# A selective scan's outputs written back into the gathered rows' tiles, and the last token rows through three tiles

## The chip, the cores and the metric

The kernel runs on one core of a Trainium2 chip. The metric is the device time of one execution in microseconds (us). The engines are named as in the profile: PE (matrix multiply; PEld its weight loads), DVE, ACT, POOL, and SP, which here only issues DMAs.

## The reference, cut to what matters

Four residual layers act on one image x of 1024 channels and 64x64 pixels, in float32. Each layer adds f(groupnorm(x)) to x. Layer 0 is a layer norm with a decaying scan over the channels; layers 1 and 3 are 1x1 convolutions. Layer 2 is the one that matters here:

```
xz   = silu(in_proj_w @ x + b);  x_ssm, res, gate = split(xz, 3)
xf   = silu(depthwise_conv3(x_ssm))             # along the 4096 tokens
dbc  = dbc_w @ xf + dbc_b                       # per head: dt, B (8), C (8)
dt   = softplus(dbc[dt])
x_h, dt, B, C = each gathered by perm           # an order of tokens per head (argsort)
h_t  = exp(dt_t * A) * h_{t-1} + dt_t * B_t * x_t      # 2 heads, 8 states, 512 channels a head
y_t  = C_t . h_t + D * x_t
y    = y gathered by the inverse of perm
out  = silu(out_proj_w @ (y * silu(gate) + res) + b)
```

## The kernel before, in words

The 1x1 convolutions are products of 1024x1024 weights with 1024x4096 pixels. They are done by one or two steps of Strassen's scheme, which trades products for sums of weights (POOL) and of inputs (DVE, POOL).

**Up to 1124 us.** Layers 0 and 1 come first. From about 590 us PE does the x_ssm product (WX). Between its parts lie the convolution, the turning of tokens into rows and a sort of the tokens by their scan order. `turn` writes each token's 512 channels of a head into a table in device memory, `tok_d` (line 1098 and its neighbours). `finish(pair)` (line 1143) is called for each of four pairs of 8 blocks of 128 tokens. It makes dt by a softplus and multiplies B by it. Then it writes for four blocks at a time (TPB) the second part of each token's row into the tile `row`. There dt stands once, and B and C in split form: `hi` holds the upper 20 bits (line 1198), `lo` the rest (line 1200), each in two places, so that one product with both gives the full precision. The second places are copied by POOL (lines 1201 and 1202). SP then sends the rows to `tok_d` (lines 1204 to 1210). A token's row has 512 + NF2 = 656 floats. There is only one `row` tile, so the next four blocks can be written only when the transfer of the last has landed. `finish` is a generator: between its `yield`s the loop does a step of the product.

**1124 to 1142 us.** The last pair is finished without product steps between (`for _ in finish(NP - 1)`). It has a ninth, partial block for the very last token.

**1142 to 1657 us, the scan.** The 4096 tokens of a head are taken in 74 chunks of 56 (8 more rows carry the state). One chunk of both heads fills a tile g of 128 rows, from a pool with 6 buffers. `gather(k)` (line 1291, POOL) fetches the rows of chunk k from `tok_d` in scan order by an indirect DMA. For iteration k the engines get this order:

- PE: `turn_rows(k+1)` (lines 1305 and 1306) turns B and C and sums dt; then a unit of the `res` product (WR, line 839, eight matmuls); `apply(k-1)` (line 1344) multiplies the chunk's weights G with its rows; `cross(k)` (line 1327) multiplies B with C; maybe another unit.
- DVE: `weigh(k-1)` (lines 1335 to 1340) makes G; `spread_decay(k+1)` (lines 1312 to 1320); sums for the product (lines 797 and 1028).
- ACT: ds, the running sums' input for chunk k+2 (line 1299); copies of finished products (line 1024); in `apply`, the state rows into the next chunk's tile (line 1347) and y out of PSUM into a tile y (line 1349); `Exp` of the decay of chunk k+1 (line 1384); Silu of finished `res` parts (line 1034).
- POOL: `scatter(k-1)` (line 1353) sends y to `y_d` by an indirect DMA to the tokens' own places; `gather(k+5)`; sums of inputs (line 797) and of weights for the next stage (lines 468 to 488).

These orders are written out by hand, so an instruction that waits holds all behind it on its engine. A scatter waits for the copy of its y and for the scatter before to land, since both write `y_d`. There are two y tiles, so the copy of y(k) waits for scatter k-2 to land. PE's products of chunk k+1 wait for gather k+1 and for ds of it. The tile y of PSUM (py) is single, so `apply(k)` waits for the copy of y(k-1).

Of the `res` product 14 units come before the first chunk (`first`); the other 98 are spread evenly over the iterations. SP's loads and stores for the product, and for the sums of weights, stand in one queue.

**From 1657 us** PE does the remaining products: gate, out_proj and layer 3.

Of the kernel before, what the change touches and what calls it, by code (L numbers as in the profile page):

```python
# [9 lines left out]
F32 = mybir.dt.float32  # L10
# [9 lines left out]
P = 128  # L20
C = 1024
HW = 64
N = HW * HW
# [13 lines left out]
NK = -(-N // LT)  # L37
HS = HEADS * S
KW, MW = 4 * HS, 66
NF2 = 9 * HS  # L40
CF, BF, DT = 0, KW, 2 * KW
HI, LO = {CF: (0, 2), BF: (0, 1)}, {CF: (1, 3), BF: (2, 3)}
NSPEC = HEADS * S + 1

W1, WX, WR, WG, WO, W3 = range(6)
# [47 lines left out]
def tile_net(ctx: ExitStack, tc: tile.TileContext, x, par_d, cst_d, w_d, w2_d, dbcw_d, out):  # L93
# [137 lines left out]
    with tc.tile_pool(name="spec", bufs=1) as sp:  # L231
        rows = sp.tile([NSPEC, DH + NF2], F32, name="spec")
        nc.gpsimd.memset(rows, 0.0)
        for at in (BF, CF):
            for j in HI[at]:
                c = DH + at + j * HS
                nc.gpsimd.tensor_copy(rows[:HS, c : c + HS], ident[:HS, :HS])
        nc.sync.dma_start(tok_d[HEADS * N :, :], rows)
# [262 lines left out]


    mean0 = const.tile([P, CT], F32, name="mean0")
    sum0 = const.tile([P, CT, 2 * NPIECE], F32, name="sum0")
    sq0 = const.tile([P, CT, 2 * NPIECE], F32, name="sq0")
    with tc.issue_after(exp_ln.ins), tc.tile_pool(name="l0x", bufs=2) as lx, \
            tc.tile_pool(name="l0x2", bufs=1) as lx2, \
            tc.tile_pool(name="wsum0", bufs=1, side="right") as wsum0, \
# [30 lines left out]
        for t in range(T0):  # L539
            nc.gpsimd.tensor_scalar(dtm[:, t, :], cst[:, CST["row"]], pcol("dtw", t), None, ALU.mult)  # L540
        carry = l0.tile([P, 2, T0], F32, name="carry", bufs=1)
        nc.vector.memset(sum0, 0.0)
        nc.vector.memset(sq0, 0.0)
        nmean0 = l0.tile([P, CT], F32, name="nmean0", bufs=1)
# [494 lines left out]
    with tc.tile_pool(name="l2a", bufs=2) as pa, tc.tile_pool(name="l2a2", bufs=1) as pa2, \  # L1039
# [11 lines left out]
        def tok_rows(t0, q, n, c0, h):  # L1051
            return tok_d[h * N + t0 : h * N + t0 + q * P, c0 : c0 + n].rearrange("(q p) c -> p q c", p=P)
# [91 lines left out]
        def finish(pair):  # L1144
            n = 2 * TPB
            yield
            acc = accs[pair].rearrange("p b (h f) -> p b h f", h=HEADS)
            if pair == NP - 1:

                nc.vector.memset(acc[:, n], 0.0)  # L1150
                nc.scalar.activation(end, end, AF.Silu)
                pe = ps_tp("end_pt")
                nc.tensor.transpose(pe[:CT, :P], end, ident)
                et = pa.tile([CT, P], F32, name="end_t", bufs=1)
                nc.scalar.copy(et, pe[:CT, :P])
                for h in range(HEADS):
                    nc.sync.dma_start(tok_d[h * N + N - 1 : h * N + N, :DH].rearrange("a (b c) -> (a b) c", c=P),
                                      et[h * KH : (h + 1) * KH, :])
                pz = ps_tp("end_dbc")
                for o in range(CT):  # L1160
                    nc.tensor.matmul(pz[:1, : HEADS * NF], end[:, o : o + 1], both[:, o, P:], start=(o == 0), stop=(o == CT - 1))
                nc.vector.tensor_tensor(accs[pair][:1, n], pz[:1, : HEADS * NF], dbcb[:1], ALU.add)
                n += 1


            def t(name):
                w = pa.tile([P, 2 * TPB + 1, HEADS], F32, tag=f"sp_{name}", name=f"sp_{name}{pair}", bufs=1)
                return w[:, :n]

            f = acc[:, :n]  # L1170
            v, m, e, u, d = t("v"), t("m"), t("e"), t("u"), t("d")
            nc.vector.tensor_copy(v, f[:, :, :, 0])
            nc.vector.tensor_scalar(m, v, 0.0, None, ALU.max)
            nc.scalar.activation(e, v, AF.Abs)
            nc.scalar.activation(e, e, AF.Exp, scale=-1.0)

            nc.vector.tensor_scalar(u, e, 1.0, None, ALU.add)
            nc.vector.tensor_scalar(d, u, -1.0, None, ALU.add)
            nc.vector.tensor_tensor(d, e, d, ALU.subtract)
            nc.vector.reciprocal(v, u)  # L1180
            nc.vector.tensor_tensor(d, d, v, ALU.mult)
            nc.scalar.activation(u, u, AF.Ln)
            nc.vector.tensor_tensor(u, u, d, ALU.add)
            nc.vector.tensor_tensor(u, u, m, ALU.add)
            nc.vector.tensor_tensor(f[:, :, :, 1 : 1 + S], f[:, :, :, 1 : 1 + S],
                                    u.unsqueeze(3).to_broadcast([P, n, HEADS, S]), ALU.mult)
            for b0 in range(0, n, TPB):
                if b0:
                    yield
                q = min(TPB, n - b0)  # L1190
                nc.vector.tensor_copy(row[:, :q, :, DT], u[:, b0 : b0 + q])
                for h in range(HEADS):
                    for at, c in ((BF, 1), (CF, 1 + S)):
                        v = f[:, b0 : b0 + q, h, c : c + S]
                        parts = row[:, :q, h, at : at + KW].rearrange(
                            "p b (a c) -> p b a c", c=HS)[:, :, :, h * S : (h + 1) * S]
                        (hi, hi2), (lo, lo2) = ([parts[:, :, j] for j in which[at]] for which in (HI, LO))
                        nc.vector.tensor_scalar(hi.bitcast(I32), v.bitcast(I32), 12, 12, ALU.logical_shift_right,
                                                ALU.logical_shift_left)
                        nc.vector.tensor_tensor(lo, v, hi, ALU.subtract)  # L1200
                        nc.gpsimd.tensor_copy(hi2, hi)
                        nc.gpsimd.tensor_copy(lo2, lo)
                    t0 = pair * 2 * FB + b0 * P - 1
                    if t0 < 0:
                        nc.sync.dma_start(tok_d[h * N : h * N + P - 1, DH:], row[1:, 0, h, :])
                        nc.sync.dma_start(tok_rows(t0 + P, q - 1, NF2, DH, h), row[:, 1:q, h, :])
                    elif q < TPB:
                        nc.sync.dma_start(tok_d[h * N + N - 1 : h * N + N, DH:], row[:1, 0, h, :])
                    else:
                        nc.sync.dma_start(tok_rows(t0, q, NF2, DH, h), row[:, :q, h, :])  # L1210

        forget(LATE)
        with tc.manual_schedule(engines={E_.DVE, E_.PE, E_.Pool, E_.Activation}):
# [60 lines left out]

    with tc.tile_pool(name="l2r2", bufs=6) as prg, tc.tile_pool(name="l2g", bufs=6) as pgat, tc.tile_pool(name="l2b", bufs=2) as pb, tc.tile_pool(name="l2h", bufs=1) as ph, \
            tc.tile_pool(name="ps2b", bufs=1, space=PSUM) as psb:
        rg_pools[:] = [prg] * 6 + rg_pools * 4
        G2 = [ph.tile([P, P], F32, name=f"G{i}") for i in range(2)]  # L1280
# [60 lines left out]

        def apply(k):
            py = psb.tile([P, FB], F32, tag="y", name=f"py{k}")
            nc.tensor.matmul(py, G2[k % 2], rows.pop(k)[:, :DH], start=True, stop=True)  # L1344
            if k + 1 < NK:
                for h in range(HEADS):
                    nc.scalar.copy(rows[k + 1][h * LC : h * LC + S, :DH], py[h * LC : h * LC + S])  # L1347
            y = pb.tile([P, DH], F32, tag="y", name=f"y{k}")
            nc.scalar.copy(y, py)  # L1349
            return y  # L1350

        def scatter(k, y):
            nc.gpsimd.indirect_dma_start(  # L1353
                out=y_d[:, :], out_offset=bass.IndirectOffsetOnAxis(ap=dst_[:, k : k + 1], axis=0),
                in_=y[:, :], in_offset=None,
            )

        sums = (None for m in (WO, W3) for _ in sum_weights2(m, ph, nc.sync, 64, lag=(1, None)))
# [3 lines left out]

        pgs = {}
        with tc.manual_schedule(engines={E_.DVE, E_.PE, E_.Pool, E_.Activation}):
            while given < first:
                next_units(total)
            for k in range(5):
                gather(k)
            step_sums(0)
            for k in range(-1, NK + 1):  # L1370
                upto = first + (k + 2) * (total - first) // (NK + 2)
                turned = turn_rows(k + 1) if k + 1 < NK else None
                if k > 0:
                    weigh(k - 1, pgs.pop(k - 1))
                if turned is not None:
                    spread_decay(k + 1, *turned)
                if k + 2 < NK:
                    step_sums(k + 2)
                next_units(upto)
                y = apply(k - 1) if k > 0 else None  # L1380
                if 0 <= k < NK:
                    pgs[k] = cross(k)
                if k + 1 < NK:
                    nc.scalar.activation(decay_[k + 1], decay_[k + 1], AF.Exp)
                if y is not None:
                    scatter(k - 1, y)
                if 4 < k + 5 < NK:
                    gather(k + 5)
                next_units(upto)
                if given // 2 % 14 != 12:  # L1390
                    next(sums, None)
                if len(silus) > 3:
                    activate(4)
# [427 lines left out]
```

## Time and profile before

| | us |
|---|---|
| median of three runs | 2715.85 (2709.34 to 2719.6) |
| the profiled execution | 2721.77, span 2719.4 |
| PE busy in the span | 2577.5 |
| the stretch of the last pair of rows | 1124 to 1142 |
| the scan | 1142 to 1657 |

A line of waits gives an instruction, what released it, the total of its waits, how many there were and the longest. A timeline line gives the start, the duration, the engine, the line of the kernel, the operation with out<-in and, in brackets, how long the engine had stood idle before and what ended that. Where the named releaser had finished long before, another event of the same wait was the last one. A row of windows gives the busy time of each engine in a stretch, the clock that PE was granted (1.00 is full), and the share of time in which the DMA engines were busy.

### The profile page before, as it was taken

How to read it: one execution, taken by the hardware profiler on the slowest of the kernel's cores; microseconds unless marked ns; L12 is line 12 of the kernel's file. 1: busy time of each engine (PE TensorE's matmuls, PEld its weight loads, DVE VectorE, ACT ScalarE, POOL GpSimd, SP SyncE). 2: the span in 40 equal slices, each digit the busy share in tenths (PEclk: the TensorE clock that was granted, in tenths of full speed). 3: DMA queues.
4: the chain of work that ended last, by engine and by line, in shares of the span. 5: the costliest groups of instructions: out<-in, count | busy, mean ns of one | idle time of the engine just before them, and what ended most of it. 6: DMA issues, size and time to landing. Idle time of an engine off the chain costs nothing.

```text
span 2719.4 us, 30951 instructions
## 1 busy us (share of the span) xinstructions
PE 2577.5 (95%) x9520; PEld 1715.8 (63%) x9520; DVE 1824.2 (67%) x3870; ACT 1086.4 (40%) x1840; POOL 1223.9 (45%) x1166
## 2 busy tenths in 40 slices
PE   4788999999999999999999999999999999999999
PEld 3664444444555555444444447888888888788887
DVE  6996856655555644377777775577576686877777
ACT  3783110103646554375766554322233133321220
POOL 4154123232122220246585665566575565654544
PEclk9897999999999999999999999999999999999999
DMA  7245467546443363478888994879799898788896
GB/s 287 102 169 201 147 218 262 190 124 230 139 138 103 110 175 111 144 236 262 236 236 236 277 269 152 242 244 305 217 278 292 235 308 238 248 304 292 299 328 215
DMA packets 423577, 598.22 MB, mean 220 GB/s; under 512 B 141909, under 2 KB 211669, under 8 KB 420342
## 3 DMA queue, kind: packets, MB, share of 16 engines
q1 hardware_dynamic: 299062, 368.89, 42.3%
q10 hardware_dynamic: 91456, 136.33, 14.3%
q0 software_dynamic: 32896, 91.04, 12.9%
q8 instruction: 77, 1.26, 0.2%
q14 instruction: 86, 0.70, 0.1%
HBM read 435.63 MB, written 160.51 MB: 219 GB/s over the span
## 4 chain that ended last, share of the span: by engine, by line
PE 48%; DVE 3%; DMA 2%; issue 2%; ACT 2%; POOL 1%; SPq 0%; DVEq 0%; POOLq 0%; ACTq 0%
PE mm L839 8%; PE q_P2P L1695 5%; PE q_P6P L1695 5%; PE q_P5P L1695 5%; PE q_P3P L1695 5%; PE q_P7P L1695 5%; PE q_P1P L1695 5%; PE q_P4P L1695 5%; PE py L1344 2%; DMA y_d<-y,dst 1%; POOL s L468 1%; PE pr L1305 1%; DMA g<-tok_d,src 0%; DVE pg L1337 0%; DVE t L797 0%
## 5 line engine op out<-in xcount | busy, mean ns | idle before, releaser
L839 PE MATMUL mm<-t,w 128*128 128x512 f32 x1536 | 687.4, 598 | 9.3 <-ACT rg L1024 6.2
L839 PE MATMUL mm<-b,w 128*128 128x512 f32 x1152 | 518.7, 602 | 4.0 <-ACT b L943 2.9
L839 PEld LDWEIGHTS mm<-t,w 128*128 128x128 f32 x1536 | 287.4, 191 | 335.2 <-issue 315.6
L839 PEld LDWEIGHTS mm<-b,w 128*128 128x128 f32 x1152 | 218.0, 193 | 254.7 <-issue 243.7
L1664 ACT COPY qQ<-q_P5P 128x512 f32<-128x512 f32 x48 | 28.1, 585 | 294.9 <-PE q_P5P L1695 294.9
L1065 DVE SCALAR_TENSOR_TENSOR cvp<-xs,par,cvp 128x512 f32<-128x512 f32 x128 | 95.3, 754 | 71.7 <-ACT cvp L1062 69.4
L1353 POOL DMA_INDIRECT y_d<-y,dst x74 | 74.9, 1012 | 143.2 <-ACT y L1349 83.5
L468 POOL TENSOR_TENSOR s<-s 128x256 f32<-128x256 f32 (+3 forms) x120 | 130.0, 1090 | 7.9
L1092 POOL TENSOR_TENSOR acc<-l2xt,acc 128x136 f32<-128x136 f32 x56 | 27.2, 486 | 234.6 <-ACT l2xt L1086 233.6
L1116 DVE TENSOR_TENSOR xs<-mm,xs 128x512 f32<-128x512 f32 x64 | 41.9, 685 | 125.0 <-PE mm L839 125.0
L1347 ACT COPY g<-py 8x512 f32<-8x512 f32 x146 | 83.6, 573 | 77.4 <-PE py L1344 69.5
L958 DVE SCALAR_TENSOR_TENSOR image<-mm,par,image 128x512 f32<-128x512 f32 x64 | 47.2, 746 | 95.6 <-PE mm L839 95.6
L1084 PEld LDWEIGHTS l2pt<-both,cv 128*128 128x128 f32 x512 | 77.6, 192 | 34.6 <-issue 24.2
L1335 DVE TENSOR_TENSOR E<-E,pg 128x512 f32<-128x512 f32 x74 | 50.5, 683 | 69.1 <-PE pg L1327 63.5
L797 POOL TENSOR_TENSOR t<-t,b 128x512 f32<-128x512 f32 x40 | 55.6, 1416 | 90.7 <-DVE t L797 90.6
L943 ACT ACTIVATE b<-image,gnl_bias,gnl_r_r 128x512 f32<-128x512 f32 x48 | 36.9, 807 | 143.8 <-PE mm L839 122.4
L1695 PE MATMUL q_P1P<-t_b,wq_P1P 128*128 128x256 f32 x384 | 92.5, 385 | 1.9 <-POOL t_b L1459 1.9
L1463 ACT ACTIVATE qb<-x_x_b,gn_bias,gn_r_r 128x512 f32<-128x512 f32 x64 | 48.8, 807 | 109.2 <-DVE qQ L1625 37.3
L1695 PE MATMUL q_P4P<-t_t,wq_P4P 128*128 128x256 f32 x384 | 90.9, 380 | 1.3 <-DVE qV L1672 1.3
L797 POOL TENSOR_TENSOR t<-b,t 128x512 f32<-128x512 f32 x60 | 76.2, 1294 | 35.4 <-DVE t L797 35.3
L1695 PE MATMUL q_P5P<-t_t,wq_P5P 128*128 128x256 f32 x384 | 90.8, 379 | 0.0
L1695 PE MATMUL q_P6P<-t_t,wq_P6P 128*128 128x256 f32 x384 | 90.7, 379 | 0.0
(418 smaller groups left out, 5972.5 us busy)
## 6 DMA issues: line engine op xcount, KB each, us to landing
w<-s_d SPq DMA_DIRECT2D x96, 512.0 KB
w<-in_w_dram SPq DMA_DIRECT2D x72, 512.0 KB
x_x_b<-x_d ACTq DMA_DIRECT2D x28, 1024.0 KB
image<-x_d SPq DMA_DIRECT2D x12, 2048.0 KB
wq_P6P<-s_d SPq DMA_DIRECT2D x84, 256.0 KB
wq_P7P<-s_d SPq DMA_DIRECT2D x84, 256.0 KB
wq_P5P<-s_d SPq DMA_DIRECT2D x84, 256.0 KB
wq_P3P<-s_d SPq DMA_DIRECT2D x84, 256.0 KB
```

The lines of the kernel that those rows point to most:

```text
L468: eng.tensor_tensor(out, a, b, ALU.subtract)
L797: eng.tensor_tensor(B[name][k], B[one][k], B[two][k], ALU.subtract)
L839: nc.tensor.matmul(to[o], w[:, k, o * P : (o + 1) * P], B[name][k], start=(fresh and k == 0), stop=(k == KH - 1), skip_group_check=True)
L958: nc.vector.scalar_tensor_tensor(part, ps, pcol(bias_name, o), part, ALU.add, ALU.add)
L1065: nc.vector.scalar_tensor_tensor(cv, xo[:, at + t : at + t + FB], pcol("dww", 3 * o + t), cv, ALU.mult, ALU.add)
L1084: nc.tensor.matmul(pt[:, q * NV : (q + 1) * NV], cv[:, (q0 + q) * P : (q0 + q + 1) * P], both[:, o, :], start=True, stop=True)
L1335: nc.vector.tensor_tensor(Ef, Ef, pg, ALU.mult)
L1344: nc.tensor.matmul(py, G2[k % 2], rows.pop(k)[:, :DH], start=True, stop=True)
L1347: nc.scalar.copy(rows[k + 1][h * LC : h * LC + S, :DH], py[h * LC : h * LC + S])
L1353: nc.gpsimd.indirect_dma_start(out=y_d[:, :], out_offset=bass.IndirectOffsetOnAxis(ap=dst_[:, k : k + 1], axis=0), in_=y[:, :], in_offset= ...
L1463: nc.scalar.activation(tile_of(j, name)[:, k], held[j, "x", name][:, k], AF.Identity, bias=bias, scale=scale)
L1695: nc.tensor.matmul(ps[:, o, :], w[:, k, o * P : (o + 1) * P], rhs[:, k, :], start=(new and o == 0 and k == 0), stop=(k == 1), skip_group_c ...
```

## The change: what it does

- A row in `tok_d` gets 642 floats in place of 656 (NF2 130 for 144). `hi` and `lo` are written into both of their places by one DVE operation each; POOL's copies go.
- The rows of the last pair are written through three tiles: `row` (4 blocks), `row4` (3) and `row7` (1 and the partial one), the two new ones in slots of the pool of `xs`, cleared by POOL. Each tile has transfers of its own. For the other pairs the second four blocks are written one product step later.
- `apply` copies y back into the tile of the gathered rows, and the scatter reads it there. The y tiles go; the pool of g has eight buffers in place of six. The copy of y stands behind `Exp` on ACT.
- The first five gathers are written ahead of the first 14 product units, and `activate(4)` is called among those units.
- `sum0` and `sq0` of layer 0 are kept in a pool of that layer.

```diff
-NF2 = 9 * HS
+NF2 = 2 * KW + 2
-HI, LO = {CF: (0, 2), BF: (0, 1)}, {CF: (1, 3), BF: (2, 3)}
+HI = {CF: slice(0, 3, 2), BF: slice(0, 2)}
+LO = {CF: slice(1, 4, 2), BF: slice(2, 4)}
...
-            for b0 in range(0, n, TPB):
-                if b0:
-                    yield
-                q = min(TPB, n - b0)
-                nc.vector.tensor_copy(row[:, :q, :, DT], u[:, b0 : b0 + q])
+            lots = [(0, TPB, row), (TPB, TPB, row)]
+            if pair == NP - 1:
+                lots = [(0, TPB, row)]
+                for b0, q in ((TPB, 3), (TPB + 3, n - TPB - 3)):
+                    w = pa.tile([P, 2 + 2 * FB], F32, tag="xs", name=f"row{b0}", bufs=4)
+                    nc.gpsimd.memset(w, 0.0)
+                    lots.append((b0, q, w[:, : 3 * HEADS * NF2].rearrange("p (b h c) -> p b h c", b=3, h=HEADS)))
+            for b0, q, to in lots:
+                if b0 and to is row:
+                    yield
+                    yield
+                nc.vector.tensor_copy(to[:, :q, :, DT], u[:, b0 : b0 + q])
                 for h in range(HEADS):
                     for at, c in ((BF, 1), (CF, 1 + S)):
-                        v = f[:, b0 : b0 + q, h, c : c + S]
+                        v = f[:, b0 : b0 + q, h, c : c + S].unsqueeze(2).to_broadcast([P, q, 2, S])
...
-                        nc.gpsimd.tensor_copy(hi2, hi)
-                        nc.gpsimd.tensor_copy(lo2, lo)
...
-tc.tile_pool(name="l2g", bufs=6) as pgat
+tc.tile_pool(name="l2g", bufs=8) as pgat
...
         def apply(k):
             py = psb.tile([P, FB], F32, tag="y", name=f"py{k}")
-            nc.tensor.matmul(py, G2[k % 2], rows.pop(k)[:, :DH], start=True, stop=True)
+            nc.tensor.matmul(py, G2[k % 2], rows[k][:, :DH], start=True, stop=True)
...
-            y = pb.tile([P, DH], F32, tag="y", name=f"y{k}")
-            nc.scalar.copy(y, py)
-            return y
+            return py, rows.pop(k)[:, :DH]
...
+            for k in range(5):
+                gather(k)
             while given < first:
                 next_units(total)
-            for k in range(5):
-                gather(k)
+                if len(silus) > 3:
+                    activate(4)
...
-                y = apply(k - 1) if k > 0 else None
+                py, y = apply(k - 1) if k > 0 else (None, None)
                 if 0 <= k < NK:
                     pgs[k] = cross(k)
                 if k + 1 < NK:
                     nc.scalar.activation(decay_[k + 1], decay_[k + 1], AF.Exp)
-                if y is not None:
+                if py is not None:
+                    nc.scalar.copy(y, py)
                     scatter(k - 1, y)
```

## The prediction

> **What bounds the kernel now.** I read the busy times first, then TensorE's waits in the stage that the change touches (1142 to 1657 us), then the order of ACT and POOL there, and last the few us before 1142.
>
> ```profile
> PE 2577.5 (95%) x9520; PEld 1715.8 (63%) x9520; DVE 1824.2 (67%) x3870; ACT 1086.4 (40%) x1840; POOL 1223.9 (45%) x1166
> ```
>
> TensorE (PE) is the bound: all that can be won is its idle time and its slow clock. PE's waits between 1142 and 1657 us (total us, times, longest us):
>
> ```profile
> PE pr L1306 <- ACT ds L1299: 9.5, 7, 2.9
> PE mm L839 <- ACT rg L1024: 6.2, 1, 6.2
> PE py L1344 <- DVE G L1340: 4.0, 5, 2.0
> PE py L1344 <- ACT y L1349: 3.1, 4, 2.1
> PE mm L839 <- POOL t L797: 2.9, 2, 1.9
> PE q_P1P L1695 <- ACT qb L1463: 2.2, 1, 2.2
> PE py L1344 <- ACT rg L1034: 1.5, 1, 1.5
> PE pr L1305 <- DMA g<-tok_d,src: 1.5, 3, 0.7
> ```
>
> With 0.6 and 0.4 in two more rows PE waits 31.9 us. The copy of y, which the change frees, holds PE itself for only 3.1 us. ACT's waits in the same stretch:
>
> ```profile
> ACT y L1349 <- DMA y_d<-y,dst: 48.2, 21, 6.4
> ACT ds L1299 <- DMA g<-tok_d,src: 23.9, 16, 5.8
> ```
>
> ACT stands 48.2 us before the copy of y, since only two y tiles exist and tile k waits for scatter k-2 to land. What releases it is seen in the timelines of ACT and then of POOL:
>
> ```profile
> 1538.70 1.16 ACT L1347 COPY g<-py 8x512 f32<-8x512 f32 x2 [2.34 <-PE py L1344]
> 1544.32 0.59 ACT L1349 COPY y<-py 128x512 f32<-128x512 f32 x1 [4.45 <-DMA y_d<-y,dst]
> ```
>
> ```profile
> 1533.78 3.55 POOL L468 TENSOR_TENSOR s<-s 128x448 f32<-128x448 f32 x3
> 1537.29 2.49 POOL L797 TENSOR_TENSOR t<-t,b 128x512 f32<-128x512 f32 x2
> 1539.94 1.00 POOL L1353 DMA_INDIRECT y_d<-y,dst  x1 [0.16 <-ACT g L1347]
> 1541.25 0.96 POOL L1291 DMA_INDIRECT g<-tok_d,src  x1 [0.30 <-issue]
> 1545.02 0.99 POOL L1353 DMA_INDIRECT y_d<-y,dst  x1 [2.81 <-ACT y L1349]
> ```
>
> Scatter 55 started at 1539.94, though its y (copied from 1526.31) had been ready 13 us: POOL was at its sums. Scatter 56 waited for 55's landing, not for y. So it goes from scatter 10 (1233.86) to 70: none starts less than 1.3 us after its copy began to lie ready. POOL's chain (sums, scatter, landing, gather) paces itself at (1648.25 - 1233.86)/63 = 6.58 us a chunk; PE's own work is about 460 us for 74 chunks, 6.2. The two are nearly level. The windows show what a gap costs besides its length (window, busy times, then granted clock, DMA share, GB/s):
>
> ```profile
> 1140.00:1160.00 20.00, 17.46 (x46) 8.73 (x47) 8.61 (x26) 8.87 (x15) 8.75 (x20) 0.85 0.68 217
> 1540.00:1560.00 20.00, 17.78 (x41) 8.33 (x40) 12.07 (x29) 7.85 (x16) 11.45 (x13) 0.83 0.88 293
> ```
>
> Behind PE's gap of 2.07 us at 1544.96 the clock is 0.53 from 1545 to 1550 and 0.79 to 1555: about 3.4 us lost.
>
> **The change part by part.** The profiled execution took 2721.77 us (span 2719.4), 5.9 above the median 2715.85; the sum is made on it and 5.9 taken off.
>
> (1) *POOL's row copies go.* 136 copies of about 0.2 us, 27 us, on an engine busy 15 to 24 of each 100 us in that stage; PE is 97 to 100% busy there. DVE's row operations stay equal in number, each twice as wide (nearest rows: 0.19 us before, 0.22 for 64x64 elements). Worth nothing, covered by DVE's own slack (41 to 57 busy of 100), except at the last rows:
>
> (2) *Last rows through three tiles.* DVE stands twice for a row transfer to land before it may write the one row tile again, and ACT's copy behind it releases PE:
>
> ```profile
> 1135.25 0.17 DVE L1191 COPY row<-sp_u 128x8 f32<-128x8 f32 x1 [1.61 <-DMA tok_d<-row]
> 1140.05 0.17 DVE L1191 COPY row<-sp_u 128x2 f32<-128x2 f32 x1 [2.39 <-DMA tok_d<-row]
> 1141.54 0.20 DVE L1200 TENSOR_TENSOR row<-acc,row 128x8 f32<-128x8 f32 x1
> ```
>
> ```profile
> 1141.90 1.07 ACT L1024 COPY rg<-mm 128x512 f32<-128x512 f32 x2 [13.10 <-DMA tok_d<-row]
> ```
>
> In the changed order the second half of tile two still waits for the landing of its first half's transfer (issued near 1132, landing 3.95 us in the row 1131.3 to 1135.2: 1136), then eight operations and the wider third tile follow: last operation near 1138.3, against 1141.74. That would free ACT 3.4 us earlier. But the new tiles lie in slots that the next rg tiles overlap, so ACT's copy now also waits until the third tile's transfers have landed. They are queued on SP behind a weight load (0.5 us of issue): out near 1139.4, landing 1.6 to 2 us, 1141.0 to 1141.4. Gain 0.5 us. Bounds: 3.4 and 1.8 of clock won (if the overlap does not hold), 2 lost (if the transfers take the 3.95). Two memsets of 128x1026 on POOL (nearest row 0.53 us for 66x512, say 1.1 each) lie in its 5.3 us of waiting ahead of 1129.85; without that cover 2.2 us. On SP there are four more DMAs of 0.25 to 0.35 us, with the gathers behind their landing, which need not be in before 1148.78.
>
> (3) *First Silus earlier, gathers written ahead of the first products.* POOL's order is the same. ACT gets four Silus (0.71 each) and one table load (1.28) ahead of 1180, where it is busy 39.6 of 58 us, and one table load less in all. PE's 1.50 at 1213.98 (on a Silu) and 0.54 behind it may go: 1.0 won taken; bounds 2.0 won, 1.3 lost (a table load in the way).
>
> (4) *y copied after Exp.* The copy starts 0.63 us later (1.9 with a table load in between). That matters only where scatters wait for y: up to chunk 9 and the last three (1639.10, 1643.62, 1648.25, each under 0.4 us after its copy's end). 0.6 lost; bounds 0 and 1.9. The py bank is free later by as much; its next writer comes one product unit (3.49 us) later.
>
> (5) *Eight tiles, y put back into its own.* ACT's 48.2 us go. Queued behind that copy are Exp, ds for chunk k+3 and rg copies; they are late next for another reason. In iteration k the copy of y(k-1) waits for scatter k-3 to land, some 4.5 us after its start. ds(k+2), some 3 us ahead of that copy, waits for gather k+2, which POOL issues 1.31 us behind scatter k-4 and which lands 3.65 to 7.04 us later: about the start of scatter k-3. Counted from the same point of the iteration, the old wait lets PE begin 1.5 us after scatter k-3 starts, the remaining one 1.0 before it to 1.7 behind. So PE may run only some 1.5 us further ahead of POOL, once, and then goes at POOL's pace. Near the end this is plain: PE waits for gather 69 itself, and is gapless from there to 1649.
>
> ```profile
> 1604.65 0.56 PE L1305 MATMUL pr<-cst,g 128*128 128x192 f32 x2 [0.30 <-DMA g<-tok_d,src]
> ```
>
> 1.5 us won taken. Upper bound: every gap of the stage but those of (2), (3) and q_P1P, 31.9 - 6.2 - 2.0 - 2.2 = 21.5, and the slow clock of four windows, (0.08 + 0.09 + 0.08 + 0.17) x 20 = 8.4: 29.9 won. Lower: 10 lost, if longer waits for gathers bring four more slow stretches of 2.5 us (between the 1.6 and the 3.4 seen).
>
> (6) *Rows of 642 floats in place of 656.* A gathered row is 2.1% shorter; were all of the landing time in the chain (60 times 5 us) proportional, 6 us won. The rows no longer start at multiples of 64 bytes. No row of this trace shows such a transfer; the gather's spread, 3.65 to 7.04 us, bounds it: 0.4 us more at each of 60 is 24 lost. I take 0, as nothing but the size is known. The Trainium skill, "DMA: Bandwidth & Descriptors", section "How a descriptor splits into AXI transactions", says that a transfer is fetched in pieces that begin at 256-byte boundaries, and that a start off the boundary costs the bytes before it. By it an old row, already off that boundary three times in four, costs on average some 85 beats of 32 bytes and a new one the same (an estimate from its rule): neither the 6 won nor the 24 lost.
>
> Moving sum0 and sq0 to another pool adds no instruction.
>
> Sum: -0.5 - 1.0 + 0.6 - 1.5 + 0 = -2.4; 2721.8 - 2.4 - 5.9 = 2713.5, told as 2713.
>
> **The rivals.** *A, faster: POOL is not the limit.* If PE's gaps within 8 us behind a long wait of ACT for y come from it, they go: 0.36, 1.43, 0.73, 1.39, 2.86, 2.07, 0.19, 1.92, 0.46, 0.50 and 2.22 = 14.1, and with them the clock lost at 1300, 1460 and 1540 (1.6 + 1.6 + 3.4 = 6.6). 20.7 in place of 1.5: 2713.5 - 19.2 = 2694. For it: these gaps do follow the long waits. Against it: six of them name a gather or ds, and POOL's chain does not wait for y. It needs the gathers to come earlier too, by lighter DMA traffic or earlier sums.
>
> *B, slower: rows off the 64-byte grid.* Gather k+5 stands in one queue ahead of scatter k, and scatter k+1 waits for that to land; without a gather between, two scatters followed each other in 3.5 us (1630.98 to 1634.47), with one in 5 or more. 0.4 us more at each of 60: 2713 + 24 = 2737. It decides from 0.28 us each (17 us).
>
> *C, slower: the gaps gather into fewer and longer ones.* PE runs into late gathers, each gap over 2 us with a slow stretch of 2.5: seven more make 2713 + 17 = 2730. Against it: gaps of 1.92 and 2.22 us at 1573 and 1580 brought none. The skill's page "TensorE: Matmul & The Clock Gate", part 1, states that the clock halves after an idle window of about 3.4 us; the gap of 2.07 us with 0.53 behind it is shorter than that, so the trace is harsher than the rule.
>
> **How the numbers follow.** Forecast 0.50, A 0.28, B 0.13, C 0.09. A time within 0.5% (13.6 us: 2702 to 2729) is about what a measurement of this kernel can tell from no change. Faster: nearly all of A and 0.05 of the forecast, 0.32. Slower: 0.12 of B and 0.06 of C, 0.18. Same: 0.50. The forecast's own range is 2702 to 2722 (its terms' bounds without the far ends of 5 and 6). For 8 in 10 it reaches to A with some 4 us beyond, 2690, and toward B to 2734, which leaves out about one in ten at each end.
>
> **What would show it.** Right: the row of ACT's y waiting for y_d gone, the row of ds waiting for the gather grown above 23.9, scatters still 6.4 to 6.6 us apart, PE's wait at the first rg copy 5 to 6 us. A is right if PE's waits in the stage fall below 15 us and the last scatter comes more than 12 us earlier after the first. B: gathers that land clearly later at the median and scatters 6.9 us or more apart. C: PE's waits for gather or ds above 20 us with more windows below 0.9 clock. I'd be wrong altogether if the stages outside 1120 to 1660 us changed their length, where I see no cause.

## The result, and the profile after

The changed kernel takes 2721.11 us in the median of 22 runs (2710.97 to 2727.60), the kernel before 2713.64 (22 runs, 2709.34 to 2720.57). The ratio is 1.0023, 95% interval 1.0014 to 1.0032: 6 us slower (the two medians lie 7.5 us apart; times behind a ratio are worked out from the ratio). I had forecast 2713, slightly faster. The time lies in my range and within the half per cent that I called "same", but it moved to the other side, and the interval leaves out 1.

The two profiled executions stand the other way round: 2721.77 us before and 2717.71 after. Each is one draw from a spread of 11 to 17 us, so their totals say nothing here. What can be read from them are stretches that come out alike in all kernels with the same code. One such stretch is shown by PE's timeline: from the first matmul for the very last token (end_pt) to the first one of the scan (pr). Before:

```profile
1124.13 0.27 PE L1153 MATMUL end_pt<-cst,end 128*8 128x128 f32 x1
1124.92 11.43 PE L839 MATMUL mm<-t,w 128*128 128x512 f32 x26
1142.54 8.81 PE L839 MATMUL mm<-t,w 128*128 128x512 f32 x16 [6.19 <-ACT rg L1024]
1151.18 0.49 PE L1305 MATMUL pr<-cst,g 128*128 128x192 f32 x2
```

After:

```profile
1121.11 0.27 PE L1154 MATMUL end_pt<-cst,end 128*8 128x128 f32 x1
1121.90 11.43 PE L840 MATMUL mm<-t,w 128*128 128x512 f32 x26
1140.97 9.99 PE L840 MATMUL mm<-t,w 128*128 128x512 f32 x16 [7.64 <-ACT rg L1025]
1150.79 0.49 PE L1312 MATMUL pr<-cst,g 128*128 128x192 f32 x2
```

The stretch is 1151.18 - 1124.13 = 27.1 us before and 1150.79 - 1121.11 = 29.7 after. PE's gap grew from 6.19 to 7.64 us, and the 16 matmuls behind it took 9.99 us instead of 8.81, at a lower clock. So the part that was to be shortened by three tiles became 2.6 us longer. DVE and ACT after show how:

```profile
1133.31 0.19 DVE L1206 TENSOR_SCALAR row<-acc 128x48 int32<-128x48 int32 x1 [2.69 <-DMA tok_d<-row]
...
1135.72 0.18 DVE L1208 TENSOR_TENSOR row<-acc,row 128x32 f32<-128x32 f32 x1
```

```profile
1140.33 1.07 ACT L1025 COPY rg<-mm 128x512 f32<-128x512 f32 x2 [13.71 <-DMA tok_d<-row]
```

The stretch itself starts 3.02 us earlier in the second profile (1121.11 against 1124.13), so times are compared from its start. DVE is done with the rows after 14.8 us (1135.90), against 17.6 before (1141.74): 2.8 us earlier. Yet ACT's copy, which releases PE, starts after 19.2 us, against 17.8 before: 1.4 us later. It waits for the landing of the last one-row transfers, and SP had sent these behind a load of weights:

```profile
1135.64 0.33 SPq L823 DMA_DIRECT2D w<-s_d  x1
1136.06 0.38 SPq L1215 DMA_DIRECT2D tok_d<-row  x1
1136.50 0.28 SPq L1217 DMA_DIRECT2D tok_d<-row  x1
```

In the scan, PE's waits after (1142 to 1657 us):

```profile
PE pr L1312 <- DMA g<-tok_d,src: 9.5, 8, 3.8
PE mm L840 <- ACT rg L1025: 7.6, 1, 7.6
PE py L1351 <- ACT g L1393: 7.0, 6, 2.2
PE mm L840 <- POOL t L798: 2.5, 1, 2.5
PE q_P1P L1703 <- ACT qb L1471: 2.2, 1, 2.2
PE py L1351 <- DVE G L1347: 2.1, 4, 0.9
PE pr L1313 <- ACT ds L1306: 2.1, 2, 1.1
PE py L1351 <- ACT rg L1035: 1.5, 1, 1.5
```

and ACT's:

```profile
ACT ds L1306 <- DMA g<-tok_d,src: 66.8, 26, 6.5
```

Without the row of the first rg copy PE waits 26.9 us here, 25.7 before (31.9 - 6.2): the waits changed their names and not their sum. ACT's 48.2 us in front of the copy of y are gone. ds now waits 66.8 us for gathers, where it had waited 23.9.

Outside the stretch two places differ alike in all profiles of the same code. One lies in the first pair. Before, DVE is held there by a row transfer, ACT and PE behind it:

```profile
805.81 0.17 DVE L1191 COPY row<-sp_u 128x8 f32<-128x8 f32 x1 [5.17 <-DMA tok_d<-row]
```

```profile
811.75 2.53 PE L1084 MATMUL l2pt<-both,cv 128*128 128x162 f32 x8 [3.00 <-ACT l2xt L1086]
```

The change writes the second four blocks of a pair one product step later, DVE does not wait, and of PE's gap 0.39 is left, with 0.26 at the next such product:

```profile
813.71 1.37 PE L1085 MATMUL l2pt<-both,cv 128*128 128x162 f32 x8 [0.39 <-ACT l2xt L1087]
```

From the first l2pt product to end_pt it is 464.7 to 467.4 us in the three kernels with the old order (the one before, numbers 8 and 9) and 461.6 to 463.4 in the other ten. So the change wins 1.3 us or more there. The other place is in the scan. ACT has a table load and Exp ahead of the copy of y, and PE waits for that copy:

```profile
1181.23 1.28 ACT L1391 ACT_TABLE_LOAD   x1
1182.53 0.63 ACT L1391 ACTIVATE E<-E 128x512 f32<-128x512 f32 x1
1183.18 0.58 ACT L1393 COPY g<-py 128x512 f32<-128x512 f32 x1
```

```profile
1183.82 1.65 PE L1351 MATMUL py<-g,G 128*128 128x512 f32 x2 [2.03 <-ACT g L1393]
```

All eleven kernels with the copy behind Exp have this gap of 2.03 us; the one before and number 9 have one of 0.5 at that place.

### The profile page after: what moved, and what is told of

The parts are those of the page before. It is cut to its first block, busy times and chain, and to the rows that moved or that the text cites. A ratio compares the mean times of both kernels' runs of the same rounds, so it can differ in the third digit from the quotient of the medians.

```text
span 2715.6 us, 30763 instructions
## 1 busy us (share of the span) xinstructions
PE 2576.0 (95%) x9520; PEld 1715.9 (63%) x9520; DVE 1823.1 (67%) x3870; ACT 1091.5 (40%) x1839; POOL 1213.8 (45%) x1096
## 4 chain that ended last, share of the span: by engine, by line
PE 80%; DVE 8%; ACT 5%; DMA 4%; issue 1%; POOL 1%; SPq 0%; DVEq 0%; POOLq 0%; ACTq 0%
PE mm L840 35%; PE q_P2P L1703 5%; PE q_P6P L1703 5%; PE q_P5P L1703 5%; PE q_P1P L1703 5%; PE q_P3P L1703 5%; PE q_P7P L1703 5%; PE q_P4P L1703 5%; PE l2pt L1085 2%; DMA g<-tok_d,src 2%; PE py L1351 2%; DVE xt L628 1%; DVE stats L550 1%; ACT xt L594 1%; ACT b L944 1%
## 5 line engine op out<-in xcount | busy, mean ns | idle before, releaser
L1672 ACT COPY qQ<-q_P5P 128x512 f32<-128x512 f32 x48 | 28.1, 585 | 293.6 <-PE q_P5P L1703 284.2
L1358 POOL DMA_INDIRECT y_d<-g,dst x74 | 74.2, 1002 | 145.5 <-ACT ds L1306 42.8
L1680 DVE TENSOR_TENSOR qV<-q_P4P,qV 128x512 f32<-128x512 f32 x96 | 64.8, 686 | 41.7 <-PE q_P4P L1703 39.8
```

Of the source, the lines that this page charges most:

```text
L1358: nc.gpsimd.indirect_dma_start(out=y_d[:, :], out_offset=bass.IndirectOffsetOnAxis(ap=dst_[:, k : k + 1], axis=0), in_=y, in_offset=None,)
L1680: nc.vector.tensor_tensor(to, ps, to, ALU.add)
```

## The experiments

All are compared with the kernel before in the same sessions. "Stretch" is the one above, "gap" PE's wait for the first rg copy in it.

**1. One tile for the last rows again.** From the changed kernel:

```diff
-            if pair == NP - 1:
-                lots = [(0, TPB, row)]
-                for b0, q in ((TPB, 3), (TPB + 3, n - TPB - 3)):
-                    ...
+            if pair == NP - 1:
+                lots.append((2 * TPB, 1, row))
...
```

> The changed kernel with one tile for the last rows again; all else of the change stays. Theory T (the last rows): after the change ACT's first rg copy waits for the landing of a one-row transfer, PE's gap there grew from 6.19 to 7.64 us and the slow clock behind it cost 1.2 us more. If T carries the loss, this kernel's gap is near 6.2 us again and the time 2.6 us or more below the changed kernel's: ratio to before 1.0000 to 1.0013. Theory S (the scan: y in its own tile) and theory P (rows of 642 floats) expect 1.0023, unchanged.

Measured: 2720.53 us, ratio 1.0019 (1.0005 to 1.0032); stretch 28.2 us, gap 7.58. The interval reaches into theory T's range, but the gap did not go back to 6.2 us, so the loss did not go with the three tiles. With one tile DVE's second wait for a row transfer is 3.87 us, against 2.39 before and 2.27 in number 7 (one tile and rows of 656):

```profile
1138.18 0.17 DVE L1195 COPY row<-sp_u 128x2 f32<-128x2 f32 x1 [3.87 <-DMA tok_d<-row]
```

**2. Two y tiles again**, and six tiles for the gathered rows. From the changed kernel, in part:

```diff
-            return py, rows.pop(k)[:, :DH]
+            rows.pop(k)
+            return py, pb.tile([P, DH], F32, tag="y", name=f"y{k}")
```

> The changed kernel with y copied into two tiles of its own again and six tiles for the gathered rows; the copy stays behind Exp. Theory S (y in its own tile lets PE run into late gathers, fewer and longer gaps) expects the loss to go: ratio 1.000, and PE's waits for gathers back from 9.5 to about 1.5 us. Theories T and P expect 1.0023 to 1.003 (the scan of the changed kernel was 3.8 us shorter in its one profile, so that without it it is longer).

Measured: 2722.29 us, 1.0028 (1.0017 to 1.0040); stretch 29.9 us. PE's waits for gathers fell to 2.9 us, but the time did not follow. y's place is not the cause: theory S falls. (The copy still stands behind Exp here.)

**3. No early Silus.**

```diff
             while given < first:
                 next_units(total)
-                if len(silus) > 3:
-                    activate(4)
```

> The changed kernel without the four early Silus (no activate among the first 14 units). Theory Q (the early Silus and their table load put ACT back between 1141 and 1150, PE's first gap after that) expects 1.000 to 1.0015; all others expect 1.0023 or, as one table load of 1.28 us comes back, 1.0028.

Measured: 2719.93 us, 1.0023 (1.0008 to 1.0038), the same as with them; stretch 30.3 us. The interval leaves theory Q its upper part (1.0008 to 1.0015), but the stretch did not become shorter.

**4. Rows of 656 floats.** One line, everything else as changed:

```diff
-NF2 = 2 * KW + 2
+NF2 = 9 * HS
```

> The changed kernel with rows of 656 floats again (NF2 144, the last 14 unused), all else of the change kept. Theory P (rows off the 64-byte grid) expects 1.000 and gathers that land sooner. Against it stand the two profiles: the median gather landed 5.16 us after its start before and 5.25 after. T and S expect 1.0023.

Measured: 2708.36 us, 0.9973 (0.9964 to 0.9982). This turns a loss of 6 us into a gain of 7. So the shorter rows carry the loss, but not as theory P had it. A packet is one piece of a transfer in the trace's records. From a gather's start to the end of its last packet of rows it is 5.30 us in the median here, 5.25 in the changed kernel and 5.02 before; over all thirteen profiles 4.99 to 5.29 with rows of 642 and 4.85 to 5.44 with rows of 656. The gathers do not care. The stretch does: it is 20.8 us, and PE's gap almost vanishes, with no slow clock behind it. PE, then ACT, of this kernel:

```profile
1122.38 0.27 PE L1154 MATMUL end_pt<-cst,end 128*8 128x128 f32 x1
...
1136.23 7.13 PE L840 MATMUL mm<-t,w 128*128 128x512 f32 x16 [1.64 <-ACT rg L1025]
1143.20 0.49 PE L1312 MATMUL pr<-cst,g 128*128 128x192 f32 x2
```

```profile
1135.59 1.07 ACT L1025 COPY rg<-mm 128x512 f32<-128x512 f32 x2 [7.70 <-DVE rg L1029]
```

Here DVE does not wait inside the second tile, and the last row transfer lands about when DVE, which ACT waits for too, is done. Two things differ from the changed kernel: the distance of the rows in the SBUF tiles (144 floats against 130) and the rows of the table in device memory (656 against 642; 656 floats are 2624 bytes, a multiple of 64, and 642 are 2568, which is none). The next two kernels change one each.

**5. Tiles 144 floats apart, table rows of 642.** From the changed kernel (NFT is 144):

```diff
-        row = pa2.tile([P, TPB, HEADS, NF2], F32, name="row", bufs=1)
+        row = pa2.tile([P, TPB, HEADS, NFT], F32, name="row", bufs=1)
...
-  nc.sync.dma_start(tok_rows(t0, full, NF2, DH, h), to[:, :full, h, :])
+  nc.sync.dma_start(tok_rows(t0, full, NF2, DH, h), to[:, :full, h, :NF2])
```

> The changed kernel with the row tiles laid out 144 floats apart again; the table in device memory keeps its rows of 642, and the transfers take 130 floats. In the changed kernel DVE's first write of head 1 into the second tile waits for the landing of head 0's transfer out of the same tile (2.69 us); with 144 floats between it does not. Theory W (that wait carries the loss): PE's gap at the first rg copy falls from 7.64 to 2 to 4 us, ratio to before 0.998 to 0.9995. Theory A (the transfers themselves land later off the 64-byte grid): ratio 1.0015 to 1.0023, the gap 6 us or more because ACT's copy still waits some 3.8 us for the last one-row transfer.

Measured: 2716.84 us, 0.9998 (0.9988 to 1.0009); stretch 26.8 us, gap 4.83: between the two theories, so that neither fault is alone. DVE's wait is gone, SP sends all rows without a pause, the last at 1134.88, ahead of the next weight load (1135.65):

```profile
1130.56 3.46 SPq L1215 DMA_DIRECT2D tok_d<-row  x5
1134.07 0.34 SPq L1217 DMA_DIRECT2D tok_d<-row  x1
1134.50 0.33 SPq L1215 DMA_DIRECT2D tok_d<-row  x1
1134.88 0.29 SPq L1217 DMA_DIRECT2D tok_d<-row  x1
1135.65 0.33 SPq L823 DMA_DIRECT2D w<-s_d  x1
```

```profile
1139.81 1.07 ACT L1025 COPY rg<-mm 128x512 f32<-128x512 f32 x2 [10.90 <-DMA tok_d<-row]
```

But ACT, which waits for the last of them, starts only 4.9 us after its issue; in number 4 that was at most 1.9. In this profile the packets themselves are slower. In each us (from the packet records, row packets only):

```
table 642 (this kernel): 1133: 549 packets of 31 ns; 1134: 362 of 55; 1135: 332 of 62; 1136: 79 of 129; 1137: 22 of 88
table 656 (number 4):    1131: 549 packets of 30 ns; 1132: 561 of 30; 1133: 542 of 31; 1134: 210 of 31
```

Packets as slow as these are seen in this one profile: in the other four kernels with a table of 642 they take 46 ns at most in the mean of any us. What all five share is a late landing. In bursts of more than 500 row packets the last signal of landing comes 0.9 to 2.1 us after the last packet; in the eight kernels with a table of 656 it comes 0.4 to 0.9 us after it, and less than in the five at each size of burst (1024 packets: 0.94 to 2.12 against 0.35 to 0.61).

**6. Tiles 130 floats apart, table rows of 656.** The pad of the table is zeroed once, at 627 us.

```diff
-    tok_d = dram.tile([HEADS * N + NSPEC, DH + NF2], F32, name="tok_d")
+    tok_d = dram.tile([HEADS * N + NSPEC, DH + NFD], F32, name="tok_d")    # NFD = 144
...
-            rows[k] = g = pgat.tile([P, DH + NF2], F32, tag="g", name=f"g{k}")
+            rows[k] = g = pgat.tile([P, DH + NFD], F32, tag="g", name=f"g{k}")
```

> The other half: the row tiles keep 130 floats, the table gets rows of 656 (its last 14 floats filled with zeros once, 8192 pieces of 56 bytes at about 600 us). Theory W: the wait inside the second tile stays, the gap 6 us or more, ratio 1.000 to 1.002. Theory A: transfers start on the 64-byte grid again, the last one lands in 1.9 us instead of 3.8, ratio 0.9973 to 0.999. If both count, this one and the one before lie between 0.9973 and 1.0023.

Measured: 2717.32 us, 1.0005 (0.9991 to 1.0019); stretch 28.1 us. As theory W expected, the wait in the second tile is there again (DVE), and the last rows stand behind the weight load on SP:

```profile
1131.87 0.19 DVE L1206 TENSOR_SCALAR row<-acc 128x48 int32<-128x48 int32 x1 [2.41 <-DMA tok_d<-row]
```

```profile
1127.11 6.65 SPq L1215 DMA_DIRECT2D tok_d<-row  x5
1133.81 0.30 SPq L1217 DMA_DIRECT2D tok_d<-row  x1
1134.20 0.33 SPq L823 DMA_DIRECT2D w<-s_d  x1
1134.62 0.38 SPq L1215 DMA_DIRECT2D tok_d<-row  x1
1135.05 0.28 SPq L1217 DMA_DIRECT2D tok_d<-row  x1
```

```profile
1138.77 1.07 ACT L1025 COPY rg<-mm 128x512 f32<-128x512 f32 x2 [13.31 <-DMA tok_d<-row]
```

The last two transfers were issued at 1134.62 and 1135.05, but their packets run from 1137.0 to 1137.9, behind the 512 KB of weights; in the changed kernel likewise, issued at 1136.06 and 1136.50, run from 1138.7 to 1139.5. Theory A had the last one landing in 1.9 us with aligned rows. It took 3.7, because of the queue, not of the grid.

**7. Rows of 656, one tile for the last rows** (numbers 1 and 4 together).

> Rows of 656 floats and one tile for the last rows again; y in its own tile, early Silus and the wide DVE writes stay. If the three tiles carry the gain of the kernel with 656 floats (0.9973; its stretch from the last row product to the first chunk was 20.8 us against 27.1 before), this one is at 0.9995 to 1.0005. If y in its own tile or the early Silus carry it, it stays at 0.997 to 0.9985.

Measured: 2715.83 us, 0.9995 (0.9984 to 1.0006); stretch 26.8 us. The gain of number 4 needs the three tiles; nothing else of the change brings it.

**8. The kernel before with y in its own tile, and nothing else.** (sum0 and sq0 moved as in the change.)

```diff
-            y = pb.tile([P, DH], F32, tag="y", name=f"y{k}")
-            nc.scalar.copy(y, py)
-            return y
+            return py, rows.pop(k)[:, :DH]
...
                 if k + 1 < NK:
                     nc.scalar.activation(decay_[k + 1], decay_[k + 1], AF.Exp)
-                if y is not None:
+                if py is not None:
+                    nc.scalar.copy(y, py)
                     scatter(k - 1, y)
```

> The kernel before with y copied back into the gathered rows' tiles, eight of them, the copy behind Exp, and nothing else of the change (sum0 and sq0 moved to make room). The theory of the prediction (POOL's chain of scatters paces the scan): ratio 0.9993 to 1.0007, and ACT's 48.2 us before y turn into waits of ds for gathers. Its rival A (the y wait makes PE's gaps): 0.993. A loss of 0.002 or more would mean that y in its own tile slows the scan.

Measured: 2720.36 us, 1.0009 (0.9997 to 1.0021); stretch 27.0 us as before. No gain; a loss of up to 5.7 us is not excluded. ACT's row for y is gone and ds waits 65.5 us for gathers, so the wait moved as forecast. Rival A (0.993) falls.

**9. The kernel before with the three tiles, and nothing else.** Rows of 656 floats, POOL's copies and y tiles as before; the edit is the `lots` of the change, with the one product step between four blocks and the next four as before.

> The kernel before with nothing but the three tiles for the last rows: rows of 656 floats, POOL's copies, y tiles and the order of the scan as before. Theory W (the stretch between the last row product and the first chunk decides, and there the waits for row transfers): the stretch falls from 27.1 to 21 to 23 us, ratio to before 0.9972 to 0.9985. If other parts of the change are needed for that gain, 0.999 to 1.0005.

Measured: 2709.63 us, 0.9976 (0.9964 to 0.9987); stretch 20.8 us, gap 1.6. The three tiles alone are worth 6.5 us (3.5 to 9.8 by the interval).

**10. Number 4 with two y tiles.**

> The changed kernel with rows of 656 floats and two y tiles again: the three tiles without y in its own tile. If y in its own tile is worth nothing (POOL's chain paces the scan), the ratio is that of the kernel with 656 floats, 0.9965 to 0.9982. If y in its own tile loses (1.0009 alone), 0.996 to 0.997; if it wins, 0.998 or more.

Measured: 2711.49 us, 0.9980 (0.9966 to 0.9994); stretch 20.8 us. Against number 4 (0.9973) the intervals overlap widely: y's place can't be told from nothing.

**11. Tiles 144 apart, table rows of 656, pieces of 520 bytes.** Numbers 5 and 6 together: it differs from 5 in the table alone, from 6 in the tiles alone, and from 4 in the pieces, 520 bytes for 576, and in the pad that is zeroed once.

> Row tiles 144 floats apart, table rows of 656, transfers of 130 floats in pieces of 520 bytes that all start on the 64-byte grid (table pad zeroed once). The table of 642 with the same tiles had its row packets slowed from about 30 to 55 to 129 ns each towards the end and the last one-row transfer landing 4.9 us after issue, against 1.9 with pieces of 576. If it is the shared 64-byte units of neighbouring rows (starts off the grid), the packets stay at 30 ns, the gap at the first rg copy is under 2.5 us and the ratio 0.997 to 0.9985. If the length of 520 bytes is enough, they slow down again, the gap is 4 to 5 us and the ratio 0.9995 to 1.0005.

Measured: 2712.27 us, 0.9982 (0.9972 to 0.9993); stretch 21.2 us. The row packets take 28 to 29 ns to the end. PE:

```profile
1124.86 0.27 PE L1154 MATMUL end_pt<-cst,end 128*8 128x128 f32 x1
...
1139.05 7.13 PE L840 MATMUL mm<-t,w 128*128 128x512 f32 x16 [1.98 <-ACT rg L1025]
1146.02 0.49 PE L1315 MATMUL pr<-cst,g 128*128 128x192 f32 x2
```

So pieces of 520 bytes are no harm when they start on the 64-byte grid. With the three tiles, four kernels form a square:

| | table rows of 642 | table rows of 656 |
|---|---|---|
| tiles 130 apart (wait inside the second tile) | 29.7 us, 1.0023 (the change) | 28.1 us, 1.0005 (number 6) |
| tiles 144 apart | 26.8 us, 0.9998 (number 5) | 21.2 us, 0.9982 (number 11) |

Either fault by itself takes back the gain of the three tiles: 5.7 us or 6.9 on top of the 21.2 (in the ratio 0.0016 and 0.0023; the intervals of numbers 5 and 11 still overlap a little). Both together cost 8.5 us in the stretch, and 0.41% or 11 us in the time. The stretch orders nearly all kernels: 20.8 to 21.2 us go with 0.9973 to 0.9982, 26.8 to 27.1 with 0.9995 to 1.0009, 28.1 to 30.3 with 1.0005 to 1.0028. The length of the scan (494 to 503 us in all thirteen profiles) does not order them.

## Why the prediction was wrong

Two terms failed: the landing of the last rows in step 2, and the 0 of step 6 for rows of 642 floats. The second weighs more: with the 14 floats back (number 4) the ratio falls from 1.0023 to 0.9973, 13 us.

**The last rows (step 2).** I took 0.5 us won, with 2 lost as the far end, and it was 2.6 lost. The path was right: the wait inside the second tile, the weight load ahead on SP, ACT's wait for the landing. The time of issue was right too: "near 1139.4" is 15.3 us behind end_pt, and it was 15.4. The landing was mis-sized, 1.6 to 2 us for 3.8 (from the last issue, 1136.50, to ACT's start, 1140.33), since the rows stood behind the weights in the queue. With the 3.95 us of my own far case the same sum gives 1.45 us lost, just the growth of the gap: the far case came true. And I counted slow clock only as a thing to be won. Compare the windows (window, busy times, granted clock, DMA share, GB/s), first before, then after, then number 4:

```profile
1140.00:1150.00 10.00, 7.46 (x14) 3.33 (x15) 3.25 (x12) 1.42 (x3) 6.84 (x18) 0.70 0.55 151
```

```profile
1140.00:1150.00 10.00, 9.03 (x15) 3.92 (x16) 1.98 (x3) 5.32 (x9) 7.44 (x12) 0.66 0.83 246
```

```profile
1140.00:1150.00 10.00, 10.00 (x30) 5.02 (x29) 5.47 (x14) 3.85 (x7) 3.83 (x4) 1.00 0.93 350
```

The gap's own length gave 1.45 us of the 2.6; the matmuls at lower clock gave the other 1.2 (9.99 - 8.81). This second part comes in steps: the 16 matmuls took 8.59 us behind a gap of 7.58 (number 1), 9.99 behind 7.64 (the change), 9.95 behind 4.83 (number 5) and 7.13 behind 1.98 or less. So differences of a us or two between stretches of 27 to 30 us are in part such steps. By the same measure I had the good case too small: where the last transfers go out ahead of the weights and land within 2.1 us, gap and clock together give 6.3 us (27.1 to 20.8), above my bound of 3.4 + 1.8.

**The rows of 642 (step 6): right on the gathers, wrong on where to look.** Gathers landed at 5.25 us in the median against 5.02, in the range of kernels with rows of 656 (4.85 to 5.44), as the 0 taken said, and rival B's mechanism (each gather 0.4 us later) did not come. But I costed the new rows only for the gathers. The same rows are written in the stretch where landing is waited for, and they lengthened DVE's waits: inside the second tile to 2.69, 3.00 and 3.48 us (the change, numbers 2 and 3) against 2.41 in number 6, and with one tile to 3.87 against 2.27. The last transfer behind the weights took 3.7 to 3.8 us with either table. The distance of 130 floats in the tile also brings the wait inside the second tile: I read it off the changed order and took it as a fact of the three tiles, without asking whether it came from the 130. The Trainium skill's page "DMA: Bandwidth & Descriptors", section "How a descriptor splits into AXI transactions", is about what a descriptor fetches; my estimate of equal beats, worked out from it, agrees with the gathers, and it does not speak of the writes, which decided.

**Eight tiles and y (step 5): the mechanism was right, the gain nothing.** The wait went from y to ds (23.9 to 66.8 us) and POOL's chain paced on: from scatter 10 (1238.36) to scatter 73 (1643.76) 6.43 us a chunk, against 6.58 before, inside the 6.4 to 6.6 that I named. The 1.5 us taken can't be seen: alone 1.0009 (0.9997 to 1.0021).

**y behind Exp (step 4): a term too small.** I said that the py bank would be free later at no cost, as its next writer comes a product unit later. Where a table load stands between, that is not late enough: the gap of 2.03 us at 1183.82 above. PE's wait for the copy of y rose from 3.1 to 7.0 us, and with two y tiles behind Exp (number 10) PE waits 11.2 us for it. It is inside the unchanged sum of the scan's waits. (The last of the three scatters that I named came 0.56 us after its copy, not under 0.4; nothing rests on it.)

**Early Silus (step 3): 1.0 us taken, none found.** PE's 1.5 us on a Silu is still in the list, and without them the ratio is the same 1.0023.

**POOL's copies (step 1).** The profile has 72 copies, some 15 us, not the 136 and 27 that I counted; POOL was free enough either way. No run leaves out the copies alone, but the three tiles give their whole gain with the copies kept (number 9).

**The other pairs (no step).** I saw no cause for another length outside 1120 to 1660 us and priced the later writing of the other pairs at nothing, without a reason. By the profiles it won 1.3 us or more near 811 us. It did not decide, but it stands against the sign I had named.

Rival C (fewer, longer gaps in the scan) did not come: the waits' sum stayed, and the window at 1540 has a clock of 0.91 after against 0.83.

## What stays open

Why the second tile's write of head 1 is made to wait for head 0's transfer with 130 floats between the rows and not with 144: the two touch different floats in both, and the first tile (four blocks) has no such wait. That writes land late when neighbouring rows share a 64-byte unit is what the square suggests; shown is only that starts on the grid take it away. Of the changed kernel's 6 us the stretch shows 2.6. The gain near 811 us makes the rest larger, the gap of 2.03 us near 1184 makes it smaller (1.5 us more than before, and in the change and numbers 2, 3 and 5 some 1.7 us of slow clock behind it); what is left has no place that single profiles can show. The scan's totals don't show even these. y in its own tile and behind Exp may hold some of it (up to 5.7 us by the interval of number 8), but a kernel with both faults mended was 0.9973 with it.

Numbers 4 and 9 beat both kernels: the change with rows of 656 floats (2708.36 us) and the kernel before with only the three tiles (2709.63).

## What to carry to other kernels

A split of one buffer into several pays only as far as what is written lands in time for whoever waits for it: look at the whole chain from the last write to the landing, at what is queued ahead of it on the DMA queue, and at every wait that the changed program has on a transfer. When a row gets shorter, cost it where it is written and how it lies in the tile, not only where it is read; a pad of 14 floats, in the table and in the tile, was worth 13 us here, of which the stretch shows 8.9. Where a wait moves from one tile to the next because another chain sets the pace, count the gain as nothing.

## What the runs showed that I had not expected

- Row packets of 520 bytes into rows of 2568 bytes took 55 to 129 ns at the tail in one profile (number 5), and 28 to 29 ns into rows of 2624 (number 11). In all five kernels with rows of 2568 bytes the landing came late: 0.9 to 2.1 us behind the last packet, against 0.4 to 0.9.
- PE's gap of 1.64 us in number 4 was followed by full clock (1.00 in 1140 to 1150 us), those of 6.19 before and 7.64 after by 0.70 and 0.66: 4.6 us less of gap made the stretch 6.3 us shorter.
- The same gap of 2.03 us near 1184 us was followed by 3.41 us of half clock in four kernels and by full clock in seven. In every trace the clock record changes only at points 3.413 us (or a multiple of it) apart. In the four kernels the gap lay whole between two such points; in the seven a point divided it, and the longer part was at most 1.82 us. Over all thirteen profiles (700 to 2600 us) no such interval at full clock in which PE idled less than 1.69 us was followed by half clock, and none in which it idled more than 1.97 us by full clock. So the gap of 1.98 us in number 11 kept its clock by little.
- Two small transfers behind one load of 512 KB on the same queue took 3.7 to 3.8 us from issue to what waited for them, against 1.8 to 2.1 ahead of it with rows of 656.
